# A four-stage conditional network on one core: opening loads and products reordered, b2a in another buffer, the last stage's matrices and outputs in another order

## The chip, the core and the metric

The kernel runs on one core of one Trainium2 chip. A core has TensorE (PE in the profile, with PEld for its weight loads), VectorE (DVE), ScalarE (ACT), GpSimd (POOL) and SyncE (SP), which mostly issues DMAs. The metric is the time of one execution on the device in microseconds. The kernel before takes 1641.43 us (median of three runs, 1639.55 to 1641.94).

## What is computed

Input x has 16 batches of 512 steps and 512 features, cond has one row of 512 features per batch. Four layers follow each other, each added to its input:

```python
x = x + L0(x, cond)   # x + x * gate: h = silu(cond @ W1.T + b1); gate = sigmoid(h @ W2.T + b2)
x = x + L1(x, cond)   # h_t = tanh(x_t @ Wx + b + h_{t-1} @ Wh), h_0 = cond; the sequence of h_t
x = x + L2(x, cond)   # f, i = sigmoid(x @ W + b); f, i = f / (f + i + eps), i / (f + i + eps)
                      # hidden = cumsum(decay to the end * i * candidate) + cumprod(f) * cond
x = x + L3(x, cond)   # ae = layernorm(cond); h = gelu(ae @ w1 + b1); A, B = halves of h @ w2 + b2
                      # x + x @ (base + A @ B.T), A and B of rank 8 for each batch
```

L0's wavelet steps cancel, so that it is x + x times the gate, and with the outer sum x times (gate + 2). L1 is a recurrence: 512 steps, each of which needs the one before. L3's 512 x 512 matrix differs for each batch.

## The kernel before

**Opening.** All loads but the bias of L1 are issued from SyncE (L212 to L222): cond, its transpose condT, the vectors, w1 and w2 of L0 (1 MB each), x0, wx and wh of L1 (1 MB each), x1 and xb, the inputs of blocks 0, 1 and 2 (256 KB each). ScalarE issues the four bias loads (L223). TensorE first opens the PSUM banks of two blocks with products of a zero tile (L190), then computes the two layers of L0 (L257); each is turned by VectorE (L267), gets its bias (L268) and goes through a sigmoid on ScalarE (L270). From the second gate comes g2, gate + 2 (L289). Eight VectorE products (L169, `gated`) multiply the first two inputs with it.

**Recurrence.** The work goes in 64 blocks of 8 steps (`for n`, `for s`). The order on TensorE, ScalarE, VectorE and SyncE is the one in which the code is written. In a step TensorE adds h @ Wh for the step (16 matrix products of 32 rows by 128 columns, two records each in the profile, L371 with wh_sb), then some of x @ Wx of the next block (L371 with wx_sb, by the table `SHARE`), and pieces of L3's factor matrices (L332) and of L2's gates (L418). ScalarE does four tanhs (L535), VectorE turns each (L536), and the turned h is the next step's operand. For block 0, x @ Wx of its first step pair is done ahead of the loop, before the first h @ Wh; for the rest of that block it follows in steps 0 to 2. `end_layer` (L346 to L356) closes a block's factor: VectorE adds the bias into the tile "got" (L347) and four DMAs store it to memory (L349); after block 0 there is a Gelu instead (L356). After block 2, `turn_bias` transposes b2a, copies it into a tile of the same tag "got", which has one buffer (L363), and stores it. From block 8 on, ScalarE also does sigmoids for L2 (L432); sigmoid and Gelu have different activation tables.

**L2 and L3.** After the recurrence, a planner orders the instructions by the order in which the code gives them and by its own estimates. For each batch b there are four gate units j (`gate_unit`): 12 products on TensorE (L591), two sigmoids (L606), ten operations on VectorE (L607 to L622: sum, reciprocal, products, three scans), and two sums on GpSimd (L626, L627) that give a quarter of x3. Part of f and i was made during the recurrence and is loaded by SyncE (L605). Tiles f, i, s and the output tile osb have two buffers each. `load_layer` loads the two factors, `make_layer` multiplies them (four small products "pl", L645) and VectorE adds the base matrix (L648). `last_layer` is x3 times the layer's matrix: four output blocks t of four products each (L655), a copy on ScalarE (L659), a store by SyncE (L660). It runs one batch late, after gate unit 1 of the next batch. The products pl and po use PSUM banks of the tags "pl" and "po", two each; the third and fourth pl product use the tag of po.

Of the kernel before, what the change touches and what calls it, by code (L numbers as in the profile page):

```python
# [30 lines left out]
F32 = mybir.dt.float32  # L31
# [4 lines left out]
P = 128  # L36
# [29 lines left out]
def made_before(b, j):  # L66

    return max(steps.stop for batches, steps, chunk in SETS if b in range(B)[batches] and chunk == j)

EPS = 1e-8  # L70
LN_EPS = 1e-5

# [5 lines left out]
def kernel(  # L78
# [24 lines left out]
    def chunks(w):  # L103
        return w.rearrange("(k p) n -> p k n", p=P)
# [98 lines left out]

    with tc.tile_pool(name="pre", bufs=1, side="right") as pre, tc.tile_pool(
        name="ps_pre", bufs=1, space=PSUM
    ) as ps_pre:
        w1_sb = pre.tile([P, KC, D], F32)
        w2_sb = pre.tile([P, KC, D], F32)  # L210
        cond_sb = pre.tile([B, D], F32)
        nc.sync.dma_start(out=cond_sb, in_=cond)  # L212
        nc.sync.dma_start(out=condT_sb, in_=chunks(condT))
        nc.sync.dma_start(out=vec_sb, in_=vecs)
        nc.sync.dma_start(out=w1_sb, in_=chunks(w1T))
        nc.sync.dma_start(out=w2_sb, in_=chunks(w2T))
        x0 = load_x(0, pre, "x0")
        nc.sync.dma_start(out=wx_sb, in_=chunks(wx))
        nc.sync.dma_start(out=wh_sb, in_=chunks(wh))
        x1 = load_x(1, pre, "x1")  # L220
        xb = load_x(2)
        for j in range(KC):  # L222
            nc.scalar.dma_start(  # L223
                out=bias_sb[j * BP : (j + 1) * BP],
                in_=l1b[:, j * BP : (j + 1) * BP]
                .rearrange("(o c) f -> o c f", o=1)
                .to_broadcast([BP, KC, BP]),
            )

        blank = pre.tile([P, 2 * P], BF16)  # L230
# [12 lines left out]
        nc.vector.tensor_scalar(var, mv[:, 1:2], LN_EPS, None, ALU.add)  # L243
        std = pre.tile([B, 1], F32)
        nc.scalar.activation(std, var, AF.Sqrt)
        rstd = pre.tile([B, 1], F32)
        nc.vector.reciprocal(rstd, std)
        xhat = pre.tile([B, D], F32)
        nc.vector.tensor_scalar(xhat, cond_sb, mv[:, 0:1], rstd, ALU.subtract, ALU.mult)
        banks = [[begin(n, i, blank) for i in range(NBANK)] for n in range(2)]  # L250

        def turned_layer(src, w_sb, which, name, between):

            ps = ps_pre.tile([P, P], F32, tag="pre", name=f"ps_{name}")
            for k in range(KC):
                for j in range(KC):
                    nc.tensor.matmul(  # L257
                        ps[j * BP : (j + 1) * BP, :],
                        src(k),
                        tile_columns(w_sb[:, k, :], j),  # L260
                        start=(k == 0),
                        stop=(k == KC - 1),
                        skip_group_check=True,
                    )
            between()
            z = pre.tile([P, KC, BP], F32, name=f"z_{name}")
            nc.vector.transpose(z, ps.rearrange("p (c f) -> p c f", c=KC))  # L267
            nc.vector.tensor_tensor(z, z, vector_of(which), ALU.add)  # L268
            gate = pre.tile([P, KC, BP], F32, name=f"gate_{name}")
            nc.scalar.activation(gate, z, AF.Sigmoid)  # L270
            return z, gate

        turned = ps_pre.tile([P, KC, B], F32, tag="ae", name="ae")

        def turn():
            for k in range(KC):
                nc.tensor.transpose(turned[:, k, :], xhat[:, k * P : (k + 1) * P], ident[:B, :B])

        def scale():
            for k in range(KC):  # L280
                nc.vector.tensor_scalar(
                    aeT[:, k, :B], turned[:, k, :], col(C_LNG, k), col(C_LNB, k), ALU.mult, ALU.add
                )

        z, gate = turned_layer(lambda k: h0[:, k, B:], w1_sb, C_L0B1, "hq", turn)
        hq = pre.tile([P, KC, BP], F32)
        nc.vector.tensor_tensor(hq, z, gate, ALU.mult)
        _, gate = turned_layer(lambda k: hq[:, k, :], w2_sb, C_L0B2, "g", scale)
        nc.vector.tensor_scalar(g2, gate[:, :, :B], 2.0, None, ALU.add)  # L289
        xs = [new_x1(0), new_x1(1)]  # L290
        for i in range(len(MOVES)):
            gated(nc.vector, xs[0], x0, i)
        for i in range(len(MOVES)):
            gated(nc.vector, xs[1], x1, i)
        nc.scalar.dma_start(out=b2a_raw[:, :, :R], in_=b2a)

    x2pool = ctx.enter_context(tc.tile_pool(name="x2pool", bufs=1, side="right"))
    x2 = x2pool.tile([P, KC, B, S], F32)
# [43 lines left out]
    def end_layer(i):  # L342
# [9 lines left out]
        else:  # L352
# [2 lines left out]
            nc.vector.tensor_tensor(z, z, vector_of(C_L3B1), ALU.add)  # L355
            nc.scalar.activation(hT3[:, :, :B], z[:, :, :B], AF.Gelu)  # L356

    def turn_bias():

        turned = ps_q.tile([P, P], F32, tag="pg", name="b2a_turned")  # L360
        nc.tensor.transpose(turned, b2a_raw.rearrange("p k r -> p (k r)"), ident)
        got = w2pool.tile([P, P], F32, tag="got", name="b2a_got")
        nc.vector.tensor_copy(got, turned)  # L363
        for c in range(KC):
            nc.sync.dma_start(out=bias_a[:, c * P : (c + 1) * P], in_=got[c * BP : c * BP + R, :])
# [125 lines left out]
    BEGINS = {T - 1: 0, 0: 1, 2: 2}  # L491

    pre, nxt = banks
    for i in range(KC):
        inputs(0, i, pre)
    for _ in range(AHEAD):
        load_chunk()
    h_prev = h0[:, :, B:]
# [1 line left out]
    for n in range(NBLK):  # L500
# [3 lines left out]
        for s in range(T):  # L504
# [28 lines left out]
            for c in range(KC):  # L533
                at = slice(c * BP, (c + 1) * BP)
                nc.scalar.activation(a[:, at], pre[bank][:, place, at], AF.Tanh)  # L535
                nc.vector.transpose(turned[:, c, :], a[:, at])  # L536
            if s == max(PAIRS[g]):
                t0, t1 = PAIRS[g]
                step = t1 - t0
                at = slice(n * T + t0, n * T + t1 + step // abs(step), step)  # L540
                nc.vector.tensor_tensor(  # L541
                    x2[:, :, :, at].rearrange("p k b t -> p k t b"),
                    xs[n][:, :, t0 // 2, :, :],
                    turned.rearrange("p k (t b) -> p k t b", t=2),
                    ALU.add,
                )
            elif n + 2 < NBLK:
                gated(nc.vector, xs[n + 2], xb, s)
                if s == G - 1 and n + 3 < NBLK:
                    xb = load_x(n + 3)  # L550
# [87 lines left out]
    def make_layer(b, at, bt, layer):  # L638
# [8 lines left out]
        for c, pl in enumerate(made):  # L647
            nc.vector.tensor_tensor(layer[:, c, :], pl, base_sb[:, c, :], ALU.add)  # L648

    def last_layer(b, x3, layer):  # L650
        for t in range(S // P):
            at = slice(t * P, (t + 1) * P)
            po = ps_o.tile([P, D], F32, tag="po", name=f"po_{b}_{t}")
            for k in range(KC):
                nc.tensor.matmul(  # L655
                    po, x3[:, k, at], layer[:, k, :], start=(k == 0), stop=(k == KC - 1)
                )
            osb = work.tile([P, D], F32, tag="osb", name=f"osb_{b}_{t}")
            nc.scalar.copy(osb, po)  # L659
            nc.sync.dma_start(out=out[b, at, :], in_=osb)  # L660

    pending = None
    for b in range(B):
        x3 = x3pool.tile([P, KC, S], F32, tag="x3", name=f"x3_{b}")
        end = b == B - 1
        if not end:
            factors = load_layer(b)
        for j in range(KC):
            gate_unit(b, j, x3)
            if j == (KC - 1 if end else 1) and pending is not None:  # L670
                last_layer(*pending)
            if j == 2 and not end:
# [4 lines left out]
        pending = b, x3, base_sb if end else layer  # L677
    last_layer(*pending)


# [56 lines left out]
```

## Time and profile before

| what | us |
|---|---|
| median of the three runs | 1641.43 |
| the profiled execution's own time | 1640.39 |
| its span, first to last instruction | 1638.6 |
| recurrence, from the first tanh to the last, starts | 18.85 to 913.04 |
| L2 and L3, from the first gate product | 914.32 to 1638.6 |

The page of the profile gives, for each engine, the busy time and its share of the span, and then the busy share in slices. Waits are given as "who <- for whom: total, times, longest". The timeline gives start, length, engine, line of the kernel, operation, output <- input, shape and count, and in brackets how long the engine had stood idle and what released it. SPq is SyncE's queue of DMA issues; the length there is the time of issuing, not of the transfer. Lengths of products on TensorE are modelled at their ends, so that starts say more than lengths. A line ending in x4 sums up four instructions.

### The profile page before, as it was taken

The page shows a single profiled execution, that of the slowest core. Times are in us where ns is not written, and L with a number is a line of the kernel's source. Part 1 is how long each engine was busy: PE and PEld are TensorE (multiplying, and loading weights), DVE is VectorE, ACT ScalarE, POOL GpSimd, SP SyncE. Part 2 cuts the span into 40 slices and gives each one's busy share as a digit, 9 for nine tenths or more (in the row PEclk, how much of TensorE's full clock was granted, in tenths as well). Part 3 has the DMA queues.
Part 4 walks back from the last instruction along what each step waited for, and adds up shares of the span by engine and source line. Part 5 has one row for each costly group of instructions (what it writes and reads, how often), then busy time and mean ns, then how long its engine had stood idle before and what let it go on. Part 6 is the DMA issues. An engine that isn't in the chain of part 4 may idle for free.

```text
span 1638.6 us, 67294 instructions
## 1 busy us (share of the span) xinstructions
PE 1610.1 (98%) x29117; PEld 1135.8 (69%) x29117; DVE 1132.8 (69%) x3592; ACT 419.3 (26%) x2476; POOL 173.0 (11%) x144
## 2 busy tenths in 40 slices
PE   7899999999999999999999999999999999999998
PEld 6788888888888888888888555555555555555553
DVE  3444655565555656566565798888888888899886
ACT  3233333333333333333333111111111111111111
POOL 0000000000000000000000022212121222222221
PEclk9999999999999999999999999999999999999999
DMA  5344432111111111111110001101111111111111
GB/s 188 112 148 144 127 108 53 36 37 36 36 33 34 36 36 36 37 36 36 36 37 23 26 23 39 41 32 41 38 41 38 44 43 43 39 34 37 44 36 57
DMA packets 106042, 86.05 MB, mean 53 GB/s; under 512 B 15072, under 2 KB 84224, under 8 KB 105744
## 3 DMA queue, kind: packets, MB, share of 16 engines
q1 hardware_dynamic: 104640, 81.66, 16.3%
q8 instruction: 228, 3.74, 0.9%
q14 instruction: 70, 0.57, 0.1%
q10 hardware_dynamic: 1104, 0.08, 0.0%
HBM read 54.95 MB, written 26.76 MB: 50 GB/s over the span
## 4 chain that ended last, share of the span: by engine, by line
PE 90%; DVE 6%; issue 2%; ACT 1%; DMA 1%; POOL 0%; SPq 0%; DVEq 0%; ACTq 0%; POOLq 0%
PE pre L371 41%; PE po L655 11%; PE pg L418 11%; PE pf L591 8%; PE pi L591 8%; PE pc L591 8%; DVE s L608 1%; PE pl L645 1%; PE pf L332 1%; DVE s L620 1%; DVE s L616 1%; DVE i L619 0%; DVE h_out L536 0%; ACT a L535 0%; DVE f L622 0%
## 5 line engine op out<-in xcount | busy, mean ns | idle before, releaser
L371 PEld LDWEIGHTS pre<-wh_sb,h_out 128*32 128x32 f32 x16384 | 456.4, 110 | 157.8 <-DVE h_out L536 154.7
L371 PE MATMUL pre<-wh_sb,h_out 128*32 128x128 f32 x16384 | 548.1, 274 | 10.4 <-DVE h_out L536 6.3
L536 DVE STREAM_TRANSPOSE h_out<-a 128x32 f32<-128x32 f32 x2048 | 264.8, 187 | 357.8 <-ACT a L535 356.7
L535 ACT ACTIVATE a<-pre 128x32 f32<-128x32 f32 x2048 | 238.0, 203 | 584.9 <-PE pre L371 584.9
L371 PE MATMUL pre<-wx_sb,x 128*32 128x128 f32 x8192 | 282.0, 274 | 2.4 <-DVE x L169 2.1
L371 PEld LDWEIGHTS pre<-wx_sb,x 128*32 128x32 f32 x8192 | 233.4, 111 | 3.2 <-issue 3.1
L655 PE MATMUL po<-layer,x 128*128 128x512 f32 x480 | 208.7, 592 | 0.8 <-POOL x L627 0.8
L591 PE MATMUL pf<-x,wf_sb 128*128 128x384 f32 (+1 forms) x512 | 170.7, 476 | 1.8 <-DVE x L541 1.3
L655 PEld LDWEIGHTS po<-layer,x 128*128 128x128 f32 x480 | 91.1, 190 | 112.0 <-issue 106.9
L591 PE MATMUL pc<-x,wc_sb 128*128 128x384 f32 (+1 forms) x512 | 168.8, 473 | 0.0
L591 PE MATMUL pi<-x,wi_sb 128*128 128x384 f32 (+1 forms) x512 | 168.8, 473 | 0.0
L608 DVE RECIPROCAL s<-s 128x384 f32<-128x384 f32 (+1 forms) x64 | 157.0, 2453 | 2.1
L591 PEld LDWEIGHTS pf<-x,wf_sb 128*128 128x128 f32 x512 | 95.7, 190 | 75.1 <-issue 17.3
L626 POOL TENSOR_TENSOR s<-s,f 128x512 f32<-128x512 f32 x63 | 86.5, 1373 | 520.4 <-DVE s L620 501.5
L591 PEld LDWEIGHTS pi<-x,wi_sb 128*128 128x128 f32 x512 | 97.3, 190 | 61.0
L591 PEld LDWEIGHTS pc<-x,wc_sb 128*128 128x128 f32 x512 | 97.3, 190 | 61.0
L541 DVE TENSOR_TENSOR x<-x,h_out 128x128 f32<-128x128 f32 x256 | 101.2, 395 | 18.7
L606 ACT ACTIVATE f<-pf,vec_sb 128x384 f32<-128x384 f32 (+1 forms) x64 | 36.4, 568 | 289.9 <-POOL s L626 142.6
L659 ACT COPY osb<-po 128x512 f32<-128x512 f32 x64 | 37.5, 585 | 263.4 <-PE po L655 122.3
L607 DVE SCALAR_TENSOR_TENSOR s<-f,i 128x384 f32<-128x384 f32 (+1 forms) x64 | 35.7, 558 | 92.0 <-ACT i L606 90.9
L579 POOL MEMSET zero<- 128x1 f32 x1 | 0.1, 98 | 915.3 <-DMA early<-ei 915.3
L627 POOL TENSOR_TENSOR x<-s,x 128x512 f32<-128x512 f32 x63 | 83.6, 1328 | 4.9
(84 smaller groups left out, 1186.9 us busy)
## 6 DMA issues: line engine op xcount, KB each, us to landing
w<-in_l3w_dram SPq DMA_DIRECT2D x68, 256.0 KB
xb<-in_xT_dram SPq DMA_DIRECT2D x64, 256.0 KB
out_dram<-osb SPq DMA_DIRECT2D x64, 256.0 KB
early<-ef SPq DMA_DIRECT2D x18, 256.0 KB
early<-ei SPq DMA_DIRECT2D x18, 256.0 KB
f<-early SPq DMA_DIRECT2D x48, 64.0 KB
i<-early SPq DMA_DIRECT2D x48, 64.0 KB
f<-early SPq DMA_DIRECT2D x16, 96.0 KB
```

What stands on the lines that cost most here:

```text
L371: nc.tensor.matmul(pre[PLACE[g][0]][j * BP : (j + 1) * BP, PLACE[g][1], :], lhsT, tile_columns(w, j), start=False, stop=False, skip_group_ ...
L418: nc.tensor.matmul(ps[c * BP : (c + 1) * BP, :].rearrange("p (b t) -> p b t", **shape), w[:, k, j * P + c * BP : j * P + (c + 1) * BP], x2 ...
L535: nc.scalar.activation(a[:, at], pre[bank][:, place, at], AF.Tanh)
L536: nc.vector.transpose(turned[:, c, :], a[:, at])
L541: nc.vector.tensor_tensor(x2[:, :, :, at].rearrange("p k b t -> p k t b"), xs[n][:, :, t0 // 2, :, :], turned.rearrange("p k (t b) -> p k ...
L591: nc.tensor.matmul(p[:, te:], w_sb[:, k, j * P : (j + 1) * P], x2[:, k, b, te:], start=(k == 0), stop=(k == KC - 1),)
L606: nc.scalar.activation(gate[:, new], p[:, new], AF.Sigmoid, bias=col(bias, j))
L608: nc.vector.reciprocal(s[:, new], s[:, new])
L626: engine.tensor_tensor(s, s, f, ALU.add)
L627: engine.tensor_tensor(x3[:, j, :], s, x2[:, j, b, :], ALU.add)
L655: nc.tensor.matmul(po, x3[:, k, at], layer[:, k, :], start=(k == 0), stop=(k == KC - 1))
L659: nc.scalar.copy(osb, po)
```

## The change

The diff has five parts.

1. *Opening.* condT, cond and the vectors are loaded from ScalarE's queue, so that w1 is the first load of SyncE's. The bias follows w1 there. wh and wx are loaded in quarters, wh ahead of x0, wx behind it. TensorE begins with ten zero products of 512 columns (`idle_products`), the banks are opened between the layers of L0, followed by two zero products, and four more follow the second layer. The zero tile is twice as wide.
2. *Block 0.* The first step's h @ Wh comes before x @ Wx of the block; the gating of the second input moves from the opening into steps 0 to 3. The opening's memory is therefore closed at step 3.
3. *Block 0's end.* After the Gelu comes a sigmoid of one column, whose result is not used.
4. *b2a.* The turned b2a goes into a tile of the tag "es", which is otherwise used from block 8 on.
5. *L3.* The matrix of batch 0 is loaded and made ahead of all gate units. last_layer of batch 0 follows gate unit 2 of batch 1 instead of 1. For the last batch, the outputs use four PSUM banks, and the first three products of all four blocks come before the fourth of each.

```diff
@@ opening @@
-        nc.sync.dma_start(out=cond_sb, in_=cond)
-        nc.sync.dma_start(out=condT_sb, in_=chunks(condT))
-        nc.sync.dma_start(out=vec_sb, in_=vecs)
+        nc.scalar.dma_start(out=condT_sb, in_=chunks(condT))
+        nc.scalar.dma_start(out=cond_sb, in_=cond)
+        nc.scalar.dma_start(out=vec_sb, in_=vecs)
         nc.sync.dma_start(out=w1_sb, in_=chunks(w1T))
-        nc.sync.dma_start(out=w2_sb, in_=chunks(w2T))
-        x0 = load_x(0, pre, "x0")
-        nc.sync.dma_start(out=wx_sb, in_=chunks(wx))
-        nc.sync.dma_start(out=wh_sb, in_=chunks(wh))
-        x1 = load_x(1, pre, "x1")
-        xb = load_x(2)
         for j in range(KC):
-            nc.scalar.dma_start(
+            nc.sync.dma_start(
                 out=bias_sb[j * BP : (j + 1) * BP],
...
+        nc.sync.dma_start(out=w2_sb, in_=chunks(w2T))
+        for k in range(KC):
+            nc.sync.dma_start(out=wh_sb[:, k, :], in_=wh[k * P : (k + 1) * P, :])
+        x0 = load_x(0, pre, "x0")
+        for k in range(KC):
+            nc.sync.dma_start(out=wx_sb[:, k, :], in_=wx[k * P : (k + 1) * P, :])
+        x1 = load_x(1, pre, "x1")
+        xb = load_x(2)
...
-        banks = [[begin(n, i, blank) for i in range(NBANK)] for n in range(2)]
+        def idle_products(n):
+            ps = ps_pre.tile([P, D], F32, tag="pre", name="idle")
+            for _ in range(n):
+                nc.tensor.matmul(ps, blank[:, :P], blank, start=True, stop=True)
...
+        idle_products(IDLE[0])
         z, gate = turned_layer(lambda k: h0[:, k, B:], w1_sb, C_L0B1, "hq", turn)
         hq = pre.tile([P, KC, BP], F32)
         nc.vector.tensor_tensor(hq, z, gate, ALU.mult)
+        banks = [[begin(n, i, blank) for i in range(NBANK)] for n in range(2)]
+        idle_products(IDLE[1])
         _, gate = turned_layer(lambda k: hq[:, k, :], w2_sb, C_L0B2, "g", scale)
+        idle_products(IDLE[2])
...
-        for i in range(len(MOVES)):
-            gated(nc.vector, xs[1], x1, i)
@@ end_layer @@
             nc.scalar.activation(hT3[:, :, :B], z[:, :, :B], AF.Gelu)
+            nc.scalar.activation(z[:, 0, :1], z[:, 0, :1], AF.Sigmoid)
@@ turn_bias @@
-        got = w2pool.tile([P, P], F32, tag="got", name="b2a_got")
+        got = w2pool.tile([P, WIDE], F32, tag="es", name="b2a_got")[:, :P]
@@ recurrence @@
-    for i in range(KC):
-        inputs(0, i, pre)
...
             if n == 0 and s < G - 1:
-                for k in range(KC):
-                    inputs(0, (s + 1) * KC + k, pre)
+                for i in range((s + (s > 0)) * KC, (s + 2) * KC):
+                    inputs(0, i, pre)
...
+            if n == 0 and s < G:
+                gated(nc.vector, xs[1], x1, (0, 2, 1, 3)[s])
@@ L2 and L3 @@
+    make_layer(0, *load_layer(0), layer)
     pending = None
     for b in range(B):
...
-        if not end:
+        if 0 < b < B - 1:
             factors = load_layer(b)
         for j in range(KC):
             gate_unit(b, j, x3)
-            if j == (KC - 1 if end else 1) and pending is not None:
+            if j == {1: 2, B - 1: KC - 1}.get(b, 1) and pending is not None:
                 last_layer(*pending)
-            if j == 2 and not end:
+            if j == 2 and 0 < b < B - 1:
                 make_layer(b, *factors, layer)
...
-    last_layer(*pending)
+    pos = [
+        pool.tile([P, D], F32, tag=tag, name=f"po_{B - 1}_{t}", bufs=2)
+        for t, (pool, tag) in enumerate(((ps_g, "pl"), (ps_g, "pl"), (ps_o, "po"), (ps_o, "po")))
+    ]
+    for t, po in enumerate(pos):
+        output_part(po, t, x3, base_sb, range(KC - 1))
+    for t, po in enumerate(pos):
+        output_part(po, t, x3, base_sb, (KC - 1,))
+        leave(B - 1, t, po)
```

`output_part` is the product loop of `last_layer` for the k given, `leave` its copy and store; IDLE is (10, 2, 4).

More of the change, by code (lines that the diff above doesn't have):

```diff
@@ L68, in made_before @@
     return max(steps.stop for batches, steps, chunk in SETS if b in range(B)[batches] and chunk == j)
+IDLE = (10, 2, 4)
 EPS = 1e-8
@@ L202, in begin @@
         return bank
-    with tc.tile_pool(name="pre", bufs=1, side="right") as pre, tc.tile_pool(
-        name="ps_pre", bufs=1, space=PSUM
-    ) as ps_pre:
+    opening = ExitStack()
+    pre = opening.enter_context(tc.tile_pool(name="pre", bufs=1, side="right"))
+    with tc.tile_pool(name="ps_pre", bufs=1, space=PSUM) as ps_pre:
         w1_sb = pre.tile([P, KC, D], F32)
@@ L228 @@
             )
-        blank = pre.tile([P, 2 * P], BF16)
+        nc.sync.dma_start(out=w2_sb, in_=chunks(w2T))
[6 more added lines that the diff above has]
+        xb = load_x(2)
+        blank = pre.tile([P, D], BF16)
         nc.gpsimd.memset(blank, 0.0)
@@ L292 @@
             gated(nc.vector, xs[0], x0, i)
-        for i in range(len(MOVES)):
-            gated(nc.vector, xs[1], x1, i)
         nc.scalar.dma_start(out=b2a_raw[:, :, :R], in_=b2a)
-    x2pool = ctx.enter_context(tc.tile_pool(name="x2pool", bufs=1, side="right"))
-    x2 = x2pool.tile([P, KC, B, S], F32)
     ps_q = rnn.enter_context(tc.tile_pool(name="ps_q", bufs=1, space=PSUM))
@@ L536 @@
                 nc.vector.transpose(turned[:, c, :], a[:, at])
+            if n == 0 and s < G:
+                gated(nc.vector, xs[1], x1, (0, 2, 1, 3)[s])
+            if n == 0 and s == G - 1:
+                opening.close()
+                x2pool = ctx.enter_context(tc.tile_pool(name="x2pool", bufs=1, side="right"))
+                x2 = x2pool.tile([P, KC, B, S], F32)
             if s == max(PAIRS[g]):
@@ L648, in make_layer, with leave, output_part @@
             nc.vector.tensor_tensor(layer[:, c, :], pl, base_sb[:, c, :], ALU.add)
+    def leave(b, t, po):
+        osb = work.tile([P, D], F32, tag="osb", name=f"osb_{b}_{t}")
+        nc.scalar.copy(osb, po)
+        nc.sync.dma_start(out=out[b, t * P : (t + 1) * P, :], in_=osb)
+    def output_part(po, t, x3, layer, ks):
+        for k in ks:
+            nc.tensor.matmul(
+                po, x3[:, k, t * P : (t + 1) * P], layer[:, k, :], start=(k == 0), stop=(k == KC - 1)
+            )
     def last_layer(b, x3, layer):
         for t in range(S // P):
-            at = slice(t * P, (t + 1) * P)
             po = ps_o.tile([P, D], F32, tag="po", name=f"po_{b}_{t}")
[L654 to L660, printed above, removed]
+            output_part(po, t, x3, layer, range(KC))
+            leave(b, t, po)
+    make_layer(0, *load_layer(0), layer)
     pending = None
@@ L676 @@
                 make_layer(B - 1, *load_layer(B - 1), base_sb)
-        pending = b, x3, base_sb if end else layer
-    last_layer(*pending)
+        pending = b, x3, layer
+    pos = [
[7 more added lines that the diff above has]
+        leave(B - 1, t, po)
 def kernel(**inputs):
```

## Prediction

> **What bounds the kernel now.** I read the page's busy shares first, then the chain of work that ended last, then the waits and the timeline of the stages that the diff touches.
>
> ```profile
> span 1638.6 us, 67294 instructions
> PE 1610.1 (98%) x29117; PEld 1135.8 (69%) x29117; DVE 1132.8 (69%) x3592; ACT 419.3 (26%) x2476; POOL 173.0 (11%) x144
> ```
>
> TensorE (PE) is the bound: 98% busy, and the busy time by stage shows 46.00 of 46.00 us in each batch from 1010 to 1562 us. So time is won or lost only where PE stands still or runs slowly, and a gap before 1562 is not won back. The gaps are at the start, in block 2, after the recurrence, and at the end. The waits of the first 80 us (total, times, longest) name three:
>
> ```profile
> PE ps_hq L257 <- DMA w_sb<-in_w1T_dram: 5.5, 1, 5.5
> ...
> DVE b2a_got L363 <- DMA factor<-got: 4.5, 1, 4.5
> ...
> PE pre L371 <- DVE x L169: 2.1, 1, 2.1
> ```
>
> The timeline (start, length, engine, line) of the first steps:
>
> ```profile
> 16.77 1.96 PE L371 MATMUL pre<-wh_sb,h_out 128*32 128x128 f32 x32
> 17.20 0.90 DVE L169 TENSOR_TENSOR x<-xb,g 128x128 f32<-128x128 f32 x4 [2.01 <-DMA xb<-in_xT_dram]
> 18.85 0.46 ACT L535 ACTIVATE a<-pre 128x32 f32<-128x32 f32 x4 [4.82 <-PE pre L371]
> 21.49 0.47 ACT L535 ACTIVATE a<-pre 128x32 f32<-128x32 f32 x4 [2.17 <-PE pre L371]
> 23.20 0.46 ACT L535 ACTIVATE a<-pre 128x32 f32<-128x32 f32 x4 [1.25 <-PE pre L371]
> ```
>
> A step is from tanh to tanh (L535). The first is at 18.85, the next two 2.64 and 1.71 later: the 32 records of a step took 1.96 us at 16.77 and 1.08 us later. Block 2:
>
> ```profile
> 60.22 0.29 DVE L347 TENSOR_TENSOR got<-pf,b 128x128 f32<-128x128 f32 x1
> ...
> 64.97 0.29 DVE L363 COPY b2a_got<-b2a_turned 128x128 f32<-128x128 f32 x1 [4.46 <-DMA factor<-got]
> ...
> 65.44 1.94 PE L371 MATMUL pre<-wh_sb,h_out 128*32 128x128 f32 x32 [4.08 <-DVE h_out L536]
> ...
> 67.44 0.47 ACT L535 ACTIVATE a<-pre 128x32 f32<-128x32 f32 x4 [5.82 <-PE pre L371]
> ```
>
> VectorE (DVE) holds everything behind a copy that waits for the store of the buffer's last user. After the recurrence, batch 1:
>
> ```profile
> 974.05 0.32 SPq L605 DMA_DIRECT2D f<-early  x1
> 974.47 0.38 SPq L660 DMA_DIRECT2D out_dram<-osb  x1
> ...
> 982.96 0.32 SPq L605 DMA_DIRECT2D f<-early  x1
> ...
> 983.33 3.26 SPq L660 DMA_DIRECT2D out_dram<-osb  x3
> 985.38 2.02 PE L645 MATMUL pl<-bt,at 8*128 8x512 f32 x8
> 985.64 0.58 ACT L659 COPY osb<-po 128x512 f32<-128x512 f32 x1 [8.39 <-DMA out_dram<-osb]
> ```
>
> Each output store stands on SyncE's queue behind a load of f, which waits for GpSimd to release f; the fourth output copy waits for the second store, and the last pl products need its bank. Here PE has one gate unit (7.74 us) between, and waits little. The end:
>
> ```profile
> 1623.61 11.43 PE L655 MATMUL po<-base_sb,x 128*128 128x512 f32 x26 [1.85 <-DVE x L627]
> ...
> 1635.12 0.58 ACT L659 COPY osb<-po 128x512 f32<-128x512 f32 x1 [2.85 <-PE po L655]
> ```
>
> [...] 1.96 against 1.08 us above, full speed about 4.9 us after 15.09 and 2.7 us after 65.44. [...] each change of table set has its load; here 1.28 us, four of them. [...] In the trace the loads run at some 390 GB/s from 5 to 19 us whichever queue sent them.
>
> **The change part by part.** Signs: minus is time won.
>
> *Start, -3.0.* The tanh at 18.85 needs both matrices. In the changed order 4.46 MB end with the last quarter of wx; before, x1 ended 4.72 MB and landed at 17.20. At 0.39 MB/us that is 0.67 earlier. w1 is issued at 0.74 instead of 2.19 (three loads left SyncE's queue), 1.45 earlier, of which I give back 0.5 for small loads that now run beside it: wx complete at 15.6. Only eight products remain, so tanh at 15.6 + 0.7 = 16.3: -2.55. SyncE's queue now issues each load past the eighth only after an earlier one landed: wh waits for w1 (about 6.5), wx's third quarter for w2 (about 9.3); w2 is still flowing then, so I charge nothing; without that cover it costs a drain, see the rivals. Zero products keep PE's clock up: the first two steps took 4.35, full-speed ones 2 x 1.70, a gain of 0.95 of which I take half, since PE is mostly waiting for quarters from 12.5 to 15.6. The ten zero products are not in the trace; the nearest row is a record of L655 (0.43): 4.3 at most, inside the 5.5 that PE waits for w1. The bank openings (1.04 in the trace) and two zero products lie beside the 1.4 us from ps_hq to ps_g, the last four beside the wait for x0: nothing, and at most 0.5 if they outlast these. The six bias copies (1.47) move on ScalarE between its two gates, 3.1 idle there: nothing. b2a's load on ScalarE's queue now waits for wh's second quarter (about 11), ahead of the first tanh: nothing unless that lands after 16. The second input's gating (0.25 a step) goes behind the transposes of DVE, 0.7 to 1.0 idle per step: nothing, but the first piece waits for x1 and the third input, which land just after wx (0.7 and 1.3 later): the transposes of the second step could be up to 0.5 late. Ends: -1.6 (all 1.45 given back) to -4.4 (nothing given back, clock up).
>
> *Sigmoid after Gelu, +1.5, and -0.8 at block 8.* Gelu's table load already stands between two tanhs (31.75 to 34.09: 2.34 against 1.64). Behind it now come a second load and a one-column activation: 1.28 + 0.20, with the tanh queued behind. In return the load at 147.75 goes: its step took 2.54 against 1.74.
>
> *b2a's buffer, -5.15.* The copy waits for PE alone. Tanhs were at 60.99, 67.44, 69.44: (6.45 - 1.65) + (2.00 - 1.65). The es buffer has no user before block 8. Next late is the tanh itself. Ends 4.8 to 5.2.
>
> *First layer matrix and the move to j == 2, +8.0.* The changed order gives: for batch 1, gate unit 2, last_layer(0), then at once the pl products of batch 1, then gate unit 3. On SyncE's queue the second store of batch 0 comes behind the f load of batch 2's unit 0, which waits for GpSimd's sum of batch 1's unit 2. DVE sets that: its first unit begins at 921.37; a unit takes 9.13 (sums at 963.24, 972.37); the first also holds four adds of 0.6 and 0.7 of waiting for products: 933.6. Six more units: 988.4. GpSimd 1.6: 990.0; f load 0.4; store to copy 2.25 (983.33 to 985.64 had 2.31); copy 0.58: 993.25. PE has meanwhile done unit (1,1) at 963.4 (bound by the same DVE pace), unit (1,2) at 971.1 and last_layer (13.74) at 984.9: it stands for some 7.3 us before the fourth pl product. Then 0.7, three units of 7.74, and 1.5 for the half clock after the gap: next last_layer at 1018.7, against 1010.66. PE is full from there, so it stays. The removed waits (0.8 at L655, 0.4 at L591) are inside this. Ends +6.5 (clock holds) to +9.5 (half clock for 6 us). DVE's four adds lie in front of this, not beside it.
>
> *Last outputs, -0.8.* Twelve of 16 products no longer wait for the last x3: PE's gap of 2.0 goes and it ends at 1633.0. But copies 2 and 3 now wait for stores 0 and 1 (two buffers, 2.25 each): store 1 issued at 1632.0, copy 3 at 1634.25 instead of 1635.12. Ends -0.7 to -2.0.
>
> Sum: -3.0 + 1.5 - 0.8 - 5.15 + 8.0 - 0.8 = -0.25. On the profiled execution's 1640.39 (span 1638.6 and 1.8 around it) that is 1640.1. The runs' median is 1.04 above this execution and they spread over 2.4; I leave the forecast at 1640.1. Its own range, from the ends taken together: 1637.3 to 1643.2.
>
> **Rivals.** *No hold-up* (1631): if the stores get through earlier, for example because f is released sooner, the +8.0 becomes -0.8 and the sum -9.05: 1631.3. For it: before, the same chain cost PE under 1 us. Against: the order of the queues is fixed, and DVE has no gap to give. *The loads run dry* (1644.3): if the waits for landings on SyncE's queue let the transfers drain twice, at wh and at wx's third quarter, each costs the 1.9 us that passed between w1's issue and its flow: +3.8, and the clock gain of 0.4 goes. It decides from 3.3 us of drain on: the sum is then 3 above before. For it: wh's issue cannot precede w1's landing. Against: w2 is 2.7 us of transfer. *The table edit does nothing* (if the set is loaded elsewhere): 0.7 less, inside the range.
>
> **How the numbers follow.** A measurement of this kernel tells about 0.2% (3.3 us) from no change. Forecast 0.63 (0.11 faster by more than that, 0.47 within, 0.05 slower), no hold-up 0.25 (all faster), drained loads 0.12 (0.02 within, 0.10 slower): 0.36, 0.49, 0.15. The range 1631.0 to 1644.5 leaves out half of each rival.
>
> **What would show it.** First tanh near 16.3; no wait of b2a_got and 1.65 between tanhs there; 3.8 at the first block's end; PE's longest gap, about 7 us, in front of a pl product before 1000, with the copy of osb waiting for out_dram; last copy less than 1 us earlier relative to PE's last batch. Wrong if that gap is below 3 us, or if the first tanh comes after 18.

## The result, and the profile after

The changed kernel takes 1648.72 us (median of six runs, 1646.72 to 1650.49) beside 1641.68 for the kernel before in the same session. The ratio is 1.0044, 95% interval 1.0033 to 1.0054. It is slower by 0.44%, where I had forecast 1640.1 and no change, and it lies outside the range. The profiled execution is the slowest of the six (1650.49, span 1648.7), so the two traces stand 10.1 us apart, more than the medians (7.0).

The page of the changed kernel: TensorE is still the bound, at the same share; its busy time has grown.

```profile
span 1648.7 us, 67334 instructions
PE 1622.9 (98%) x29132; PEld 1138.6 (69%) x29133; DVE 1132.6 (69%) x3592; ACT 420.8 (26%) x2477; POOL 172.4 (10%) x144
```

**Start.** The timeline of the changed kernel (start, length, engine, line; L225 is w2's load, L237 the copy of condT, L382 the products of a step, L544 tanh):

```profile
6.71 0.39 SPq L225 DMA_DIRECT2D w_sb<-in_w2T_dram  x1
6.75 0.24 POOL L237 COPY h_out<-condT_sb 128x64 f32<-128x64 f32 x1 [4.68 <-DMA condT_sb<-in_condT_dram]
...
12.41 1.93 PE L266 MATMUL ps_g<-w_sb,hq 128*32 128x128 f32 x32 [1.26 <-DMA w_sb<-in_w2T_dram]
16.56 1.73 PE L382 MATMUL pre<-wh_sb,h_out 128*32 128x128 f32 x32
...
19.30 0.47 ACT L544 ACTIVATE a<-pre 128x32 f32<-128x32 f32 x4 [3.91 <-PE pre L382]
```

The first tanh is at 19.30, not at 16.3; before, it was at 18.85. condT, 32 KB, now beside w1, landed at about 6.7, and in that moment SyncE issued w2. TensorE waits for w2 until 12.41. The next tanhs are at 21.53 and 23.25 (before 21.49 and 23.20): the start gained nothing. Five later traces have the same opening, with the second tanh at 21.53 to 23.14, and one more has the old opening, with 21.11: single traces of a start differ by that much, and the one above is not worse than the others of the changed opening.

**Block 2.** The copy of b2a (L374) directly follows VectorE's add and waits for nothing:

```profile
62.70 0.29 DVE L355 TENSOR_TENSOR got<-pf,b 128x128 f32<-128x128 f32 x1
62.91 0.28 DVE L374 COPY b2a_got<-b2a_turned 128x128 f32<-128x128 f32 x1
63.47 0.47 ACT L544 ACTIVATE a<-pre 128x32 f32<-128x32 f32 x4 [1.05 <-PE pre L382]
```

**After the recurrence, batch 1.** L621 loads f, L668 is the output copy, L669 the store, L661 the pl products, L607 the next gate unit:

```profile
990.60 0.32 SPq L621 DMA_DIRECT2D f<-early  x1
...
990.97 3.23 SPq L669 DMA_DIRECT2D out_dram<-osb  x3
...
993.25 0.59 ACT L668 COPY osb<-po 128x512 f32<-128x512 f32 x1 [8.21 <-DMA out_dram<-osb]
993.89 2.07 PE L661 MATMUL pl<-bt,at 8*128 8x512 f32 x2 [5.02 <-ACT osb L668]
995.89 5.35 PE L607 MATMUL pf<-x,wf_sb 128*128 128x384 f32 x8
```

This is the hold-up that I had drawn up: the copy waits 8.21 for a store that left SyncE only behind the load of f, and TensorE stands 5.02. But the two pl products then take 2.07 and the eight of pf 5.35, where an undisturbed pf takes 2.74. The output layer of batch 1 starts at 1021.72, before at 1010.66.

**End.** The last batch's products start at 1630.08 and end without a gap; the third copy waits for a store:

```profile
1630.08 13.90 PE L673 MATMUL po<-base_sb,x 128*128 128x512 f32 x32
...
1644.22 0.59 ACT L668 COPY osb<-po 128x512 f32<-128x512 f32 x1 [1.30 <-DMA out_dram<-osb]
1645.12 0.59 ACT L668 COPY osb<-po 128x512 f32<-128x512 f32 x1 [0.31 <-DMA out_dram<-osb]
```

From the output layer of batch 14 (1605.29, now 1616.35) to the last copy it is 1.1 shorter.

Where the 10 us between the two traces lie, read from the starts of tanhs, products and the last copy, rounded:

| place | after minus before, us | predicted |
|---|---|---|
| start, to the eighth tanh | +0.2 | -3.0 |
| last step of block 0 (second table load) | +1.5 | +1.5 |
| block 2 (b2a) | -5.2 | -5.15 |
| block 8 (table load gone) | -0.8 | -0.8 |
| rest of the recurrence | +2.5 | 0 |
| first gate product to output layer of batch 1 | +12.8 | +8.0 |
| end | -1.1 | -0.8 |

### The profile page after: what moved, and what is told of

The parts are those of the page before. It is cut to its first block, busy times and chain, and to the rows that moved or that the text cites. A ratio compares the mean times of both kernels' runs of the same rounds, so it can differ in the third digit from the quotient of the medians.

```text
span 1648.7 us, 67334 instructions
## 1 busy us (share of the span) xinstructions
PE 1622.9 (98%) x29132; PEld 1138.6 (69%) x29133; DVE 1132.6 (69%) x3592; ACT 420.8 (26%) x2477; POOL 172.4 (10%) x144
## 4 chain that ended last, share of the span: by engine, by line
PE 94%; DVE 2%; issue 1%; DMA 1%; ACT 1%; POOL 0%; SPq 0%; ACTq 0%; POOLq 0%; DVEq 0%
PE pre L382 41%; PE po L673 12%; PE pg L429 11%; PE pf L607 9%; PE pi L607 9%; PE pc L607 9%; PE pl L661 1%; PE pf L340 1%; DVE s L624 0%; DMA out_dram<-osb 0%; DVE h_out L545 0%; DMA condT_sb<-in_condT_dram 0%; ACT a L544 0%; DMA w_sb<-in_w2T_dram 0%; POOL s L642 0%
## 5 line engine op out<-in xcount | busy, mean ns | idle before, releaser
L382 PEld LDWEIGHTS pre<-wh_sb,h_out 128*32 128x32 f32 x16384 | 458.6, 110 | 153.7 <-DVE h_out L545 150.0
L382 PE MATMUL pre<-wh_sb,h_out 128*32 128x128 f32 x16384 | 553.4, 273 | 6.7 <-DVE h_out L545 3.0
L544 ACT ACTIVATE a<-pre 128x32 f32<-128x32 f32 x2048 | 238.2, 202 | 581.1 <-PE pre L382 581.1
L382 PE MATMUL pre<-wx_sb,x 128*32 128x128 f32 x8192 | 284.4, 273 | 2.3 <-issue 2.3
L382 PEld LDWEIGHTS pre<-wx_sb,x 128*32 128x32 f32 x8192 | 235.2, 110 | 4.0 <-issue 3.8
L607 PE MATMUL pf<-x,wf_sb 128*128 128x384 f32 (+1 forms) x512 | 173.3, 482 | 1.4 <-DVE x L557 1.3
L607 PE MATMUL pi<-x,wi_sb 128*128 128x384 f32 (+1 forms) x512 | 171.4, 478 | 0.0
L607 PE MATMUL pc<-x,wc_sb 128*128 128x384 f32 (+1 forms) x512 | 168.8, 473 | 0.0
L607 PEld LDWEIGHTS pf<-x,wf_sb 128*128 128x128 f32 x512 | 96.9, 192 | 75.9 <-issue 20.9
L607 PEld LDWEIGHTS pi<-x,wi_sb 128*128 128x128 f32 x512 | 98.1, 192 | 63.7 <-issue 3.2
L607 PEld LDWEIGHTS pc<-x,wc_sb 128*128 128x128 f32 x512 | 97.5, 190 | 61.4 <-issue 0.6
L668 ACT COPY osb<-po 128x512 f32<-128x512 f32 x64 | 37.5, 586 | 257.8 <-PE po L673 135.9
L623 DVE SCALAR_TENSOR_TENSOR s<-f,i 128x384 f32<-128x384 f32 (+1 forms) x64 | 35.3, 552 | 96.3 <-ACT i L622 96.3
```

What stands on the lines that cost most here:

```text
L382: nc.tensor.matmul(pre[PLACE[g][0]][j * BP : (j + 1) * BP, PLACE[g][1], :], lhsT, tile_columns(w, j), start=False, stop=False, skip_group_ ...
L607: nc.tensor.matmul(p[:, te:], w_sb[:, k, j * P : (j + 1) * P], x2[:, k, b, te:], start=(k == 0), stop=(k == KC - 1),)
```

## The experiments

Two things were to be explained: why the start gained nothing, and why the hold-up cost half as much again as predicted. My theory for the start: the ninth load (w2) waits until the first (condT) has landed, and the transfers run dry. The rival: the half clock of TensorE (granted 0.50 to 0.51 from 8 to 18 us in the trace of after). For L3: the hold-up is the chain copy, store, load of f, GpSimd. The rival: the early matrix delays VectorE, and the store is only the wait that was seen last. All times below are ratios to the kernel before, with their 95% interval; the stage in question is read from the trace.

### Rows first (s_rows_first)

```diff
-        nc.scalar.dma_start(out=condT_sb, in_=chunks(condT))
-        nc.scalar.dma_start(out=cond_sb, in_=cond)
-        nc.scalar.dma_start(out=vec_sb, in_=vecs)
+        nc.sync.dma_start(out=cond_sb, in_=cond)
+        nc.sync.dma_start(out=condT_sb, in_=chunks(condT))
+        nc.sync.dma_start(out=vec_sb, in_=vecs)
```

> The changed kernel, with the loads of cond, condT and vec back at the head of SyncE's queue (before w1); everything else as changed. Theory (w2 is issued at 6.71 instead of about 2.5 because it stands behind condT's landing, and the transfers run dry from 5.6 to 8.4): condT lands by 3.5, w2 goes out near 5.0, nothing runs dry; 4.46 MB from about 4.2 at 0.39 MB/us end at 15.6, the first tanh comes at 16.4 instead of 19.30, and the time is 2.9 under the changed kernel's, near 1.0027 of the kernel before. Rival (the half clock of TensorE from 8 to 18 us, from the idle stretch before ps_hq, sets the first tanh): tanh not before 18, gain under 1.3.

Measured: 1.0037 (1.0023 to 1.0052). condT's copy runs at 3.13, w2 is issued at 4.63, and TensorE is at full clock when the products of the first step begin (32 in 1.08 us at 15.47). The first tanh comes at 18.80, the second at 20.57, against 19.30 and 21.53: 1.0 won, not 2.9. Neither theory holds: the dry stretch is gone (361 GB/s from 5.6 to 8.4), but the last quarter of wx still came at 18.25, and the step's products waited for it with TensorE at full clock.

### w2 second (s_w2_second)

```diff
         nc.sync.dma_start(out=w1_sb, in_=chunks(w1T))
+        nc.sync.dma_start(out=w2_sb, in_=chunks(w2T))
         for j in range(KC):
...
-        nc.sync.dma_start(out=w2_sb, in_=chunks(w2T))
```

> The changed kernel, with w2's load directly behind w1's on SyncE's queue, ahead of the four loads of bias_sb: w2 no longer stands behind condT's landing, the fourth bias load does, and wh behind it. condT stays on ScalarE's queue. If condT's landing at 6.7 has nothing to do with what is queued on SyncE: wh goes out at 7.2, no dry stretch, first tanh near 16.8, 2.5 under the changed kernel. If its rows of 64 bytes come through only when the large loads let them: it lands near 8.5 (when w2 ends), wh runs dry instead of w2, first tanh near 18.7, gain about 0.6.

Measured: 1.0045 (1.0031 to 1.0060). condT's copy ran at 6.78, as in the changed kernel, although w2 now flowed behind w1 without a break: the rows, issued at 0.74, did not wait for the large loads to end, and landed 6 us after their issue beside w1 alone as beside both. The busy time by stage from 5.6 to 8.4 us, in the changed kernel first; the last two columns are the busy share of the DMA engines and GB/s, the one before them TensorE's clock, which the second trace has no record of before 14 us:

```profile
5.60:8.40 2.80, 1.36 (x32) 0.91 (x32) 1.14 (x4) 0.37 (x2) 1.52 (x8) 0.88 0.42 52
```

With w2 second:

```profile
5.60:8.40 2.80, 1.49 (x29) 1.24 (x32) 0.99 (x3) 0.15 (x1) 1.51 (x8) 1.00 1.05 370
```

The stretch with only 52 GB/s was real, and moving w2 fills it. The first tanh still comes at 18.87, the second at 20.64: 0.9 won. Something else holds back wx.

### x1, xb and the chunks held back (s_x_late)

Rows first, and:

```diff
         xb = pool.tile([P, KC, T, B], F32, tag=tag, name=f"xb_{n}", bufs=1)
+        if after is not None:
+            nc.vector.tensor_copy(xb[:, 0, 0, 0:1], after)
...
-        x1 = load_x(1, pre, "x1")
-        xb = load_x(2)
...
         nc.vector.tensor_scalar(g2, gate[:, :, :B], 2.0, None, ALU.add)
+        x1 = load_x(1, pre, "x1", g2[:, 0, 0:1])
+        xb = load_x(2)
```

> The changed kernel, with the loads of cond, condT and vec first on SyncE's queue, and with the loads of x1, xb and the first three chunks of L3 held back until g2 is there (a copy of one column of g2 into x1's tile stands ahead of x1's load). With the rows first alone, nothing ran dry and yet the last quarter of wx landed only at 18.1. Theory (x1, xb and the chunks, issued from 12.85 on, share the engines with the last quarters of wx): without them wx is complete near 16.4, first tanh near 16.9. Rival (the quarters are slow by themselves, through their own issue waits): wx at 18 as before, first tanh at 18.8. Either way the second input is later and block 0's later steps may wait for x1 (it lands near 18.5), so the whole need not gain.

Measured: 1.0036 (1.0024 to 1.0048). The products of wx with rows first alone:

```profile
18.25 1.30 PE L382 MATMUL pre<-wx_sb,x 128*32 128x128 f32 x40 [1.04 <-DMA wx_sb<-in_wx_dram]
18.80 0.47 ACT L544 ACTIVATE a<-pre 128x32 f32<-128x32 f32 x4 [3.67 <-PE pre L382]
```

And with the later loads held back:

```profile
17.00 1.30 PE L384 MATMUL pre<-wx_sb,x 128*32 128x128 f32 x40 [0.25 <-DMA wx_sb<-in_wx_dram]
17.55 0.47 ACT L546 ACTIVATE a<-pre 128x32 f32<-128x32 f32 x4 [3.48 <-PE pre L384]
```

The last quarter of wx comes 1.25 earlier; the theory expected 1.9. The second tanh is at 19.32, 2.2 under the changed kernel. So the loads behind wx on the same queue did delay it. How much is less sure: the products of the second gate, too, began 0.47 earlier than with rows first alone (11.93 against 12.40), before x1 was issued in either, so part of the 1.25 may lie between two executions. In the overall time the gain can't be told from none; stalls of TensorE in the recurrence (see below) vary by more from trace to trace.

### Without the zero products (s_no_idle)

```diff
-IDLE = (10, 2, 4)
+IDLE = (0, 0, 0)
```

> The changed kernel without its sixteen products of zeros (ten, two, four). If they keep the clock up where it matters: the second step (2.23 between the first two tanhs in the trace of after, 1.77 with rows first) is 2.6 as in before, and the time 0.5 to 1 longer. If they matter not at all, or cost: first tanh at 19.3 or earlier, time within 0.5 of the changed kernel's.

Measured: 1.0044 (1.0031 to 1.0058), the same as the changed kernel. The step from first to second tanh is 3.03 (20.43 to 23.46) instead of 2.23, and its 32 products with wh take 1.54 (at 21.78), where they take 1.08 at full clock. The second tanh comes 1.9 later than in the changed kernel. The overall times, with an interval of 2 us to either side, do not tell the two apart.

### Output layer of batch 0 back (h_last_at_1)

```diff
-            if j == {1: 2, B - 1: KC - 1}.get(b, 1) and pending is not None:
+            if j == (KC - 1 if end else 1) and pending is not None:
```

> The changed kernel, with the output layer of batch 0 back behind unit 1 of batch 1 instead of unit 2; the first layer matrix stays ahead of the first gate unit. Theory (hold-up: the fourth output copy waits for a store that stands behind a load of f that waits for GpSimd's sum of unit 2 of batch 1): the store comes 9.1 earlier, PE no longer stands (5.0 in the trace of after) and is not at half clock afterwards (2.6), pl's products shrink from 8.2 to 2.1; gain about 9.1, against 3.7 left to the early matrix: 0.9987 to 1.0000 of the kernel before. Rival (the early matrix puts VectorE 5 us late and slows PE; the place of the output layer matters little): gain under 3.

Measured: 0.9984 (0.9977 to 0.9990), 0.6% under the changed kernel: some 9.8 us. From the first gate product to the output layer of batch 1 it is 97.9 us instead of 109.1, and TensorE stands nowhere in it. The theory holds.

### First matrix back (h_matrix_late), and both back (h_both_back)

```diff
-    make_layer(0, *load_layer(0), layer)
...
-        if 0 < b < B - 1:
+        if not end:
             factors = load_layer(b)
...
-            if j == 2 and 0 < b < B - 1:
+            if j == 2 and not end:
```

> The changed kernel, with the first layer matrix back behind unit 2 of batch 0 (loads and products); the output layer of batch 0 stays behind unit 2 of batch 1. Theory (hold-up): VectorE's four adds lie ahead of the sum of unit 2 of batch 1 either way, only their waits for products (3.0) go: sum at 986.0 + 1.6, copy at 990.3 instead of 993.25, gain about 3.0, and PE still stands, for some 8 us. Rival (the early matrix is what costs): gain 10 or more, no gap of PE.

> The changed kernel, with both edits at the start of L3 taken back: the first layer matrix behind unit 2 of batch 0 and the output layer of batch 0 behind unit 1 of batch 1; the other edits stay. From the first gate product to the next output layer (batch 1) before took 96.3 us, after 109.1, the changed kernel with only the output layer moved back 97.9, with only the matrix moved back 107.9. Theory (the hold-up is the place of the output layer; the early matrix costs 1.6 by itself): 96.3 here, 1.6 under the kernel with only the output layer moved back, so 0.9965 to 0.9985 of the kernel before. Rival (the matrix moved back costs when the output layer stands early, as it saved nothing when it stood late): 98 or more, no better than 0.9984.

Measured: with the matrix back alone 1.0057 (1.0040 to 1.0074) and 107.9 us in that stage; with both 0.9977 (0.9966 to 0.9987) and 96.25, as before the change (96.34). The matrix back alone did not bring the 3.0 that I expected: VectorE's first waits for products went, but a wait of 1.8 for a sigmoid took the place of part of them, and GpSimd's sum came at 76.3 after the first gate product (in the trace of after at 76.7). The early matrix costs 1.6 by itself. The late output layer costs 9.8 by the overall times with the early matrix and 13 without it, 11.2 and 11.6 in the traces.

### Three output buffers (m_three_osb)

```diff
-        osb = work.tile([P, D], F32, tag="osb", name=f"osb_{b}_{t}")
+        osb = work.tile([P, D], F32, tag="osb", name=f"osb_{b}_{t}", bufs=3)
```

> The changed kernel with three buffers for osb instead of two, and nothing else: the fourth output copy of batch 0 then waits for store 0 and no longer for store 1; queues and order stay. Theory (the chain of the hold-up is copy, store, load of f, GpSimd): store 0 was issued at 982.06 in the trace of after, before PE was done with the output layer, so no wait is left: from the first gate product to the next output layer 96 to 99.5 instead of 107.4 to 109.1, and at the end copy 2 no longer waits for a store, 1 more: 0.9965 to 0.9985 of the kernel before. Rival (VectorE, 9.13 per unit, is what PE really waits for; the store was only the last to be seen): the wait moves to pl or pf behind VectorE, 104 or more, gain 5 or less.

Measured: 0.9981 (0.9974 to 0.9988). The same place in the trace, with the queue in the same order:

```profile
987.39 1.91 PE L661 MATMUL pl<-bt,at 8*128 8x512 f32 x8
987.54 0.59 ACT L668 COPY osb<-po 128x512 f32<-128x512 f32 x1 [2.89 <-PE po L673]
...
989.23 2.85 PE L607 MATMUL pf<-x,wf_sb 128*128 128x384 f32 x8
...
990.83 1.39 SPq L669 DMA_DIRECT2D out_dram<-osb  x3
```

The stores leave SyncE as late as ever (990.83), but the fourth copy no longer needs one: it waits for TensorE alone, and TensorE goes on at once. The stage takes 100.3 instead of 109.1, just above the 96 to 99.5 that I expected (TensorE was at half clock from 926 to 932 here; granted from 918 to 936: 0.81), and the end is 0.9 shorter. This is the direct proof of the chain: one buffer more takes the whole wait away, with VectorE at the same pace.

### b2a's buffer alone, in the kernel before (b_b2a_only)

```diff
-        got = w2pool.tile([P, P], F32, tag="got", name="b2a_got")
+        got = w2pool.tile([P, WIDE], F32, tag="es", name="b2a_got")[:, :P]
```

> The kernel before, with the copy of the turned b2a in the es buffer and nothing else of the change. Theory: the copy waits for PE alone, 5.15 us between the tanhs of block 2 go, nothing later is late by it: 1636.5, 0.9968 of the kernel before. Rival (what is loaded meanwhile, and the stores in front of it on SyncE's queue, are late next): part of it comes back as a wait within 10 us, gain 3 or less.

Measured: 0.9973 (0.9962 to 0.9984), some 4.4 us by the ratio. The steps of block 2 that took 6.45 and 2.00 take 1.65 and 1.64, with no wait; nothing is late next. In its trace the rest of the recurrence stood longer, so that the first gate product comes only 0.6 earlier than in the trace before. TensorE's waits for "issue" (no other engine and no transfer of data that the profile could name) from 22 to 914 us; total, times, longest. Before:

```profile
PE pre L371 <- issue: 1.6, 4, 0.7
```

With b2a's buffer alone:

```profile
PE pre L371 <- issue: 4.8, 6, 1.3
```

The changed kernel without zero products:

```profile
PE pre L382 <- issue: 0.5, 1, 0.5
```

A step with such a stall takes 2.6 instead of 1.65: one of 0.67 at 45.58 in the second trace lies between tanhs at 44.32 and 46.93:

```profile
45.58 0.43 PE L371 MATMUL pre<-wx_sb,x 128*32 128x128 f32 x8 [0.67 <-issue]
```

The stalls differ in number and length from trace to trace, but not freely in place: the step from the 103rd tanh to the next (near 198 us) has one in 13 of the 14 traces, the step from the 15th (near 45 us) in 11. No run was made to find their cause, but the traces point to one. The page of every trace counts 228 transfers of 16 KB on the queue named "instruction" (the line of the trace of after):

```profile
q8 instruction: 228, 3.74, 1.0%
```

That is one for every 256 of the instructions of TensorE (58423 in the trace of after, those of its sequencer counted). All 83 stalls of the 14 traces (0.18 us or more) stand at the same place in such a group of 256, at number 192 to 194 in order of start, and end 1.2 to 1.7 us after the last byte of one of these transfers; such a transfer starts 5.0 us after the one before it (median), and 4.0 is usual from 22 to 260 us. So TensorE very probably waited for its own instructions. None of the stalls is later than 258 us; the page of after shows 106 to 186 GB/s in the slices up to 247 us, and mostly 36 from 288 us on. What makes the transfers late was not tested.

### Without the extra sigmoid (no_extra_sigmoid)

```diff
             nc.scalar.activation(hT3[:, :, :B], z[:, :, :B], AF.Gelu)
-            nc.scalar.activation(z[:, 0, :1], z[:, 0, :1], AF.Sigmoid)
```

> The changed kernel without the one-column Sigmoid behind Gelu. Theory: the step at the end of block 0 takes 2.34 instead of 3.87, the step at block 8's first ef takes 2.54 instead of 1.74 (one table load of 1.28 comes back there): net 0.7 less, 1.0040 of the kernel before beside 1.0044. Rival (the sigmoid is hidden by PE's own work there): both steps shorter or unchanged, difference 0 or against it. The overall times can't tell the two apart, the two steps in the trace can.

Measured: 1.0047 (1.0034 to 1.0060). The last step of block 0 takes 2.34 instead of 3.86, the step at block 8's first sigmoid 2.53 instead of 1.73, with a table load of 1.28 at 143.50 that the changed kernel has at 34.45: the terms are right, and the extra sigmoid costs 0.7 net in the trace. The overall times do not tell 0.7 apart.

### What the runs speak for (best_two_osb, best_three_osb)

Rows first, x1 and what follows held back, no extra sigmoid, both edits at the start of L3 taken back; b2a's buffer and the last outputs as changed; in the second, three buffers for osb as well.

> All that the runs so far speak for: the rows first, x1, xb and the L3 chunks held back until g2, no extra sigmoid, both edits at the start of L3 taken back, b2a's copy in es and the last outputs as changed. By the terms: start 2.0 under before (second tanh 19.3 against 21.5), b2a 5.15, last outputs 1.0, no change elsewhere: 8.2 less, 0.9950. Rival (the start's gain is eaten by the stalls of PE in the recurrence that no engine and no transfer explains, 0.5 to 4.8 from trace to trace): no better than the kernel before with the b2a edit alone, 0.9973.

> The same with three buffers for osb. Theory: only the end changes, where copy 2 of the last batch no longer waits for store 0 (1.3 idle in front of it in the trace of after): 0.9 less, 0.9945. Rival: the wait moves to copy 3 and to the stores, no difference from two buffers.

Measured: 0.9962 (0.9948 to 0.9975) and 0.9946 (0.9932 to 0.9960). The second takes 1633.22 us (1630.98 to 1634.47), 8.4 under the kernel before and faster than both kernels. The first run does not decide against its rival, 0.9973, which its interval just holds, and the intervals of the two runs overlap. Second tanhs at 19.75 and 19.61. In the traces the third buffer brings more than the end alone, as I had not expected: the stage after the recurrence is 95.3 instead of 96.3, since the copies there no longer wait for stores either, and the end is 0.9 shorter.

## Why the prediction was wrong

It failed in two terms of its sum; the rest of the gap between the two traces is of a kind that it did not have.

*Start, -3.0 predicted, +0.2 measured: the step failed.* It said that each load past the eighth goes out only after an earlier one landed, "wh waits for w1 (about 6.5), wx's third quarter for w2". The trace of after shows such waits: w2, the ninth load, was issued at 6.71, after 3.2 of waiting for condT, the first; wx's third quarter, the seventeenth, at 12.29, after 1.2 for w2. My sum left out the ninth load itself, and I had the small loads cost w1 half a microsecond without asking when they would land beside it. I took it that a load loses nothing when it changes its queue, and called the rate the same "whichever queue sent them", where ScalarE's queue had sent 0.08 of the 5.95 MB. condT landed at 6.7, 3.6 later than at the head of SyncE's queue, and the engines moved only 52 GB/s from 5.6 to 8.4. The first tanh, at 19.30, is behind the 18 that I had named as the sign of being wrong. My rival "the loads run dry" had the right kind of event, at two other places. A second part failed too: I let the loads end in their order, 4.46 MB at 0.39 MB/us. With no dry stretch wx came at 18.25, and at 17.0 when the loads behind it were held back. Mending both brought the second tanh 2.2 forward.

*Sigmoid, +1.5 and -0.8; b2a, -5.15; last outputs, -0.8: right.* 1.5, 0.8, 5.2 and 1.1 in the traces, the sigmoid and b2a also by a run without or with them alone. For the outputs no run was made by itself; the end, from the output layer of batch 14 to the last copy, takes 28.8 in the changed order with two output buffers, and in the old one 29.8 (before) and 31.7 (b2a's buffer alone, with a gap of 2.05 on TensorE).

*Hold-up, +8.0 predicted, +12.8 in the trace: the mechanism was right, the size was not.* The chain of queues was shown by the place of the output layer (h_last_at_1) and by the third buffer (m_three_osb). Counted from the first gate product, I had the fourth copy end at 78.9, with VectorE's adds waiting 0.7 for the early pl products. That term was too small even at full clock: in the five traces in which TensorE ran these products at full clock and the hold-up follows, the adds waited 1.7 to 1.8 and the copy ended at 79.9. In the trace of after TensorE fell to half clock there (the last four took 2.07 instead of 1.13), the adds waited 3.0 and the copy ended at 81.2, 2.3 late. Then came 2.0 for the last two pl products instead of 0.7, and 2.6 of half clock in pf instead of 1.5. That is 4.7 of the 4.8. In the seven traces that have the hold-up the stage takes 107.0 to 109.1, median 107.8, against my 104.4 and 96.3 before: a typical hold-up is 11.5, 3.5 above my term and 2 above its upper end. Of these 3.5, some 1.0 is the adds' wait and the rest TensorE at half clock behind the gap, which I had priced, by an estimate, at 1.5, for the gate products alone. Among the seven, only the trace of after had the early pl products at half clock.

*Rest of the recurrence, 0 predicted, +2.5 in the trace.* These are for the most part the stalls for "issue", with what each costs its step: 2.7 us in the trace of after against 1.6 before. Their sum varies between traces from 0.5 to 4.8, whatever the edit. So I count this term to the two executions that were profiled and not to the change. With a typical hold-up of 11.5 and without this term the table comes to 6.1, beside 7.0 between the medians.

What sets the half clock off was not shown. It came behind the gap: in the trace of after TensorE stands from 988.9 to 993.9, the granted clock is 0.50 from 990.7 to 1001.0, and pf takes 5.35; behind gaps of 5.35 to 6.99 in three others (s_rows_first, s_w2_second, h_matrix_late) it takes 4.48 to 5.49, against 2.74. But it came without a gap of that length too: ahead of the early pl products TensorE stood at most 1.34, and yet the granted clock from 918 to 936 us was 0.81 in the traces of after (0.50 from 925.9 to 932.7) and of three output buffers, 0.91 in two others (s_rows_first, h_last_at_1), and 1.00 in four, all with the same instructions there.

## What to carry to other kernels

Before a load is moved, count the loads in flight: find the one whose landing the next issue waits for, and ask when that one lands beside its new neighbours; a small load among those in flight can hold back a megabyte (here condT's 32 KB held w2 for 3.2 us). Where a copy waits for a store, look at what stands ahead of the store on its queue; a third buffer was worth as much here as the old order of the output layer (0.9981 and 0.9984). And price a gap on TensorE with the slow clock behind it: here a gap of 5.0 us came with 3.9 more in the products that followed.

## What was not expected of the hardware

- A load of 32 KB in rows of 64 bytes landed some 2 us after its issue when it went first (condT issued at 1.18, copied at 3.13), and 6 us after it beside a 1 MB load from the other queue (0.74 to 6.75), whether or not a second megabyte followed. In that time the packets of the two queues came nearly one for one: the trace of after has from 3 to 5 us 318 packets of SyncE's queue (0.65 MB) and 308 of ScalarE's (0.02 MB). Whether this is what held the rows back was not tested. ScalarE's queue is not slow by itself: before, it moved 308 packets in one microsecond, from 2 to 3, while SyncE's carried small loads only.
- wx's last quarter came at 18.25 with x1, xb and three chunks issued behind it on the same queue, and at 17.0 with these held back; part of the 1.25 may lie between the two executions. How later loads can delay an earlier one is open.
- Around the small pl products of batch 0 (8 rows) TensorE fell to half clock in four of eight traces, for 6.8 us in the trace of after (granted 0.50 from 925.9 to 932.7), with no gap longer than 1.34 us ahead. That these products are the cause was not tested.
- TensorE stood for "issue" for 0.5 to 4.8 us in a recurrence of 890 us, always at the same place in a group of 256 of its instructions and 1.2 to 1.7 us after a 16 KB transfer of instructions. What makes these transfers late is open; all the stalls lie in the stretch with the most other transfers. For a kernel that is bound by a chain of steps this varies between single traces by more than the gains of 1 to 2 us that were looked for.
